# Second tile of each later pair transposed by small SBUF transfers and VectorE instead of TensorE

## The chip, the cores and the metric

The kernel runs on one core of one Trainium2 chip. A core has TensorE (PE in the profile; PEld is its loading of stationary operands), VectorE (DVE), ScalarE (ACT), GpSimd (POOL), and SyncE (SP), which here only issues DMA transfers. The metric is the device time of one execution in microseconds. Beside the plain timings there is one profiled execution, and all durations below come from its trace.

## The reference

The input `x` has two sequences of 1024 tokens with 1024 features, all float32. The block is pre-norm attention followed by a pre-norm feed-forward layer (FFN):

```
x = x + attention(layernorm(x))     # conv of width 3, 16 heads, blocks of 128 tokens, projection
x = x + ffn(layernorm(x))

ffn(x): y = x @ W_base.T + b_base   # 1024 x 1024
        z = x @ A[active].T         # 4 experts of rank 8
        alpha = softmax(log(prior[active]) + router logits[active])
        return y + 2 * sum_e alpha_e * (z_e @ B_e.T)
```

The change touches only the FFN, and in it only how the normalized tokens get their features onto the partitions, which the product with `W_base` needs.

## The kernel before, in words

The first 500 us do the convolution and attention. The last 250 us are the FFN, over the 2048 tokens as 16 tiles of 128 tokens, taken as 8 pairs, `m` = 0 to 7. A pair is a matrix of 256 tokens by 1024 features, seen as two by two blocks: A11 and A12 are the two feature halves of the first tile, A21 and A22 those of the second. The product with `W_base` uses seven block products in place of eight (Winograd's form). It needs the sums S1 = A21 + A22, S2 = S1 - A11, S3 = A11 - A21 and S4 = A12 - S2. Each block and sum is split into a high and a low float32r part (`op_hi` L1249 on ScalarE, `op_lo` L1252 on VectorE), and a block product is three times four matmuls of 512 columns (`multiply_half`, L1271).

For a pair TensorE does, in this order: the attention projection of the next pair's second tile (`project`, tile `pp`), product 1, the projection of the next pair's first tile, product 6, product 2, the eight transposes of the next pair's second tile, product 5, the expert and router products (`pz`), product 7, the eight transposes of the next pair's first tile, product 3, the small expert products, product 4. So each pair's operands are made while TensorE works at the pair before. Products 2 and 3 use the weight blocks B21 and B22, which do not stay in SBUF. `stream` fetches each of them again for every pair as two transfers of 1 MB (`load_half`, L1123, issued by SP) into two buffers of the tag `vh`, and product 3's B22 can be fetched only when product 2 has used up B21. The trace names both `wb_B`: the matmuls `py_a<-wb_B` are product 2, `py_e<-wb_B` product 3.

A tile's way to its operands is as follows. SP loads the residual (`load_xr`, L1171). GpSimd adds the projection's bias (`add_projb`, L1174), and later in two instructions the pair's common term (`add_u`, L1377 and L1379). VectorE adds the projection (`residual`, L1189), takes the moments (`x_stats`, L133 to L1194), GpSimd the reciprocal root (`x_rstd`, L1199), and VectorE writes the normalized tile `xn` (`x_norm`, L1204). TensorE then transposes eight blocks of 128 by 128 into two PSUM banks `trx` (`transpose_x`, L1211). Of the second tile, ScalarE copies A21 out of PSUM (`keep_a21`, L1233), and VectorE adds S1 from it and from A22 (`sum_s`, L1243). A result leaves PSUM by VectorE's `add_y` (L1385), and SP stores the tile (L1413). The gate of the experts (`gate_logits`, `gate_exp`, `gate`, L1315 to L1346) stands on VectorE and ScalarE between product 7 and the small expert products.

The order on all five engines is written by the kernel itself. Each piece of work is an `Op` with an engine, an estimated duration, a due time and its predecessors, and `trace()` sorts all of them by a small list scheduler and issues them. `places` counts free buffers by tag: `m` for the eight PSUM banks, `a4` for SBUF tiles of 4 KB a partition. `port=True` tells the scheduler that a VectorE and a GpSimd instruction must not overlap. A transfer takes one of eight completion counters of SP's queue in turn, and waits until the transfer eight places before it on that queue has landed. Every engine works strictly in its order.

Of the kernel before, what the change touches and what calls it, by code (L numbers as in the profile page):

```python
# [16 lines left out]
ALU = mybir.AluOpType  # L17
# [4 lines left out]
P = 128  # L22
# [17 lines left out]
def preln_block_kernel(  # L40
# [19 lines left out]
    nc = tc.nc  # L60
    N, L, D = x.shape
# [10 lines left out]
    E = lora_b.shape[0] // R  # L72
# [577 lines left out]
    DVE, ACT, PE, DMA = "DVE", "ACT", "PE", "DMA"  # L650
# [4 lines left out]
    loaded, gs, gone = {}, {}, {}  # L655
# [7 lines left out]
    at = [14.0]  # L663
# [3 lines left out]
    def turn(i, h):  # L667

        due = at[0]
        if h == 0:  # L670
            how = HOW[i]
            if how == "scalar":
                o = Op(ACT, 1.3, due - 8.0, 8.0, [loaded[i]], partial(ln_sum, i))
                o = Op(ACT, 1.2, due - 6.0, 8.0, [o], partial(ln_square, i))
                o = Op(DVE, 0.1, due - 4.5, 8.0, [o], partial(ln_variance, i), lag=1.8)
            else:
                lag = 1.0 if how == "vector" else 1.8
                o = Op(DVE, 1.6, due - 5.5, 8.0, [loaded[i]], partial(ln_stats, i), lag=lag)
            e, us = (DVE, 0.75) if how == "vector" else (ACT, 1.15)
            seen[i] = Op(e, us, due - 2.2, 8.0, [o], partial(ln_scale, i))  # L680
        o = Op(
            PE, TR, due, 6.0, [seen[i], banks[-2] if len(banks) > 7 else None],
            partial(transpose, i, h),
        )
        if (i, h) == (8, 0):

            gone["even"] = Op(
                DMA, 0.01, due - 2.0, 50.0, [seen["tr", j, 1] for j in range(8)], even_tokens
            )
        after = [o] + ([gone["even"]] if i > 7 else [])  # L690
        seen["tr", i, h] = o
        banks.append(Op(ACT, 0.52, due + TR, 8.0, after, partial(transposed, i, h)))
        at[0] += TR
        seen[i, h] = banks[-1]
# [36 lines left out]
    for q, (v, n, dc) in enumerate(units):  # L731
# [10 lines left out]
        o = Op(DVE, 1.28, due - 5.5, 9.0, took, partial(unit_sum, q))  # L742
        o = Op(ACT, 0.55, due - 3.5, 9.0, [o], partial(unit_hi, q))
        side = Op(DVE, 0.64, due - 1.5, 9.0, [o], partial(unit_lo, q))
        for i in range(2):
            d = dc + i
# [4 lines left out]
            for c in range(NCC):  # L751
                after = [last, side, ready[v, d]]
# [48 lines left out]
    for v, dc in [(v, dc) for v in (1, 2, 3) for dc in range(0, NDC, 2)] + [(4, 0), (4, 2)]:  # L801
        if (v, dc) == (2, 0):

            for r in range(4):
                load(
                    at[0] + r, 3.0, nc.sync.dma_start, mask[r::4], causal[ts(r, P // 4)],
                    after=[last],
# [4 lines left out]
        side = begin_step(v, dc, at[0])  # L812
# [18 lines left out]
    for c in range(NCC):  # L831
        got = load(
            at[0] - 4.0, 8.0, tokens_load, 0, c, t3, NV - 1,
            after=[gone["m", v, c] for v in (0, 5, 1, 2, 3)],
# [4 lines left out]
        o = Op(DVE, 2.7, at[0] + 1.0, 6.0, [got, gone[4, c]], partial(tokens_join, 0, c))  # L839
        o = Op(ACT, 0.6, at[0] + 4.0, 6.0, [o], partial(tokens_hi, 0, c))  # L840
# [23 lines left out]
    def a4(name, shape, dt=F32):  # L864
        return ap_.tile([P, *shape], dt, tag="a4", name=name, bufs=A4)
# [197 lines left out]
    NH = NDC // 2  # L1063
# [149 lines left out]
            xns.pop(g)  # L1213


    AT = {(0, 0): "A11", (0, 1): "A12", (1, 0): "A21", (1, 1): "A22"}

    def operand(m, n):
# [6 lines left out]
    def s_of(m, n):  # L1225

        k = m, n in ("S2", "S4")
        if k not in sums:
            sums[k] = a4(f"s{int(k[1])}_{m}", (2, NH, P))
        return sums[k][:, int(n in ("S3", "S4"))]  # L1230
# [3 lines left out]

    def sum_s(m, n):
        g0, g1 = gs[2 * m : 2 * m + 2]
        a, b, how = {
            "S1": (trxs.get((g1, 1)), s_of(m, "S3"), ALU.add),
            "S2": (s_of(m, "S1"), trxs.get((g0, 0)), ALU.subtract),
            "S3": (trxs.get((g0, 0)), s_of(m, "S3"), ALU.subtract),  # L1240
            "S4": (trxs.get((g0, 1)), s_of(m, "S2"), ALU.subtract),
        }[n]
        nc.vector.tensor_tensor(s_of(m, n), a, b, how)  # L1243
# [175 lines left out]
    MM = 1.37  # L1419
    LAG = 0.25  # L1420
    ROOM = 1.09
    NI = NCHUNK * NHP
    places.update(
        m=[0.0] * 8, t2=[0.0] * 6, t4=[0.0] * 6, a4=[0.0] * (A4 - 1), ml=[0.0] * 2, vh=[0.0] * 2,
# [3 lines left out]
    gs = [ch * NB + b for ch in (2, 3, 0, 1) for b in range(NB)]  # L1428
    d = {}

    def pe(key, takes, after, f, lead=8.0, need=("m",), give=()):
        d[key] = Op(PE, takes, at[0], lead, [d.get(a) for a in after], f, need=need, give=give)
        at[0] += takes
        return d[key]

    def op(key, e, takes, due, after, f, lead=14.0, **kw):
        if e in (DVE, ACT):
            kw.setdefault("lag", LAG)
            takes *= ROOM
        d[key] = Op(e, takes, due, lead, [d[a] for a in after if a in d], f, **kw)  # L1440
        return d[key]
# [93 lines left out]
    def plan_p(n):  # L1535
        g = gs[n]
        ch = g // NB
        plan_x(n, at[0])

        if ch < NCHUNK - 2 and g % NB == 1:  # L1540
            for wc in range(NWC):
                op(("oh", ch, wc), DMA, 1.4, at[0] - 8.0, [("os", ch, wc)], partial(load_oh, ch, wc),
                   lag=3.0, need=("t4",), lead=6.0)
                d["ol", ch, wc] = d["oh", ch, wc]
        for h in range(2):
            pe(("P", n, h), MM,
               [("ol", ch, wc) for wc in range(NWC)] + [("rl", "pw", wc, h) for wc in range(NWC)],
               partial(project, g, h), give=("t4",) * 2 if h and g % NB == NB - 2 else ())
            op(("r", n, h, 0), DVE, 0.6, at[0] + 0.5, [("P", n, h), ("xb", n)],
               partial(residual, g, h), give=("m",))  # L1550
        op(("xs", n), DVE, 1.6, at[0] + 2.0, [("r", n, 0, 0), ("r", n, 1, 0)], partial(x_stats, g))
        op(("xp", n), POOL, 0.3, at[0] + 3.5, [("xs", n)], partial(x_rstd, g), lag=0.3)
        op(("xn", n), DVE, 0.75, at[0] + 5.0, [("xp", n)], partial(x_norm, g), need=("a4",), port=True)

    def plan_tx(m, t, h):

        n, o = 2 * m + t, AT[t, h]
        pe(("TX", n, h), 0.44, [("xn", n)], partial(transpose_x, gs[n], h), give=("a4",) if h else ())
        d["A", m, o] = d["TX", n, h]
        due = at[0]  # L1560

        def more(key, e, takes, dt, after, f, **kw):
            op((key[0], m, *key[1:]), e, takes, due + dt, [(a[0], m, *a[1:]) for a in after], f, **kw)

        if o == "A21":
            more(("c", o), ACT, 0.5, 0.5, [("A", o)], partial(keep_a21, m), need=("a4",), give=("m",))
        else:
            more(("h", o), ACT, 0.5, 0.5, [("A", o)], partial(op_hi, m, o), need=("a4",))
            more(("l", o), DVE, 0.6, 1.2, [("h", o)], partial(op_lo, m, o))
        made = {n for n in ("A11", "A12", "A21", "A22") if ("A", m, n) in d}  # L1570

        def split(n, dt, after):
            more(("h", n), ACT, 0.5, dt, [("s", n)], partial(op_hi, m, n), need=("a4",))
            more(("l", n), DVE, 0.6, dt + 0.7, [("h", n)], partial(op_lo, m, n), port=True)

        def done(n, dt, after):
            more(("x", n), DVE, 0.0, dt, after, partial(drop, m, n), give=("m",))

        def free(n, dt, after):
            more(("f", n), DVE, 0.0, dt, after, int, give=("a4",))  # L1580

        if {"A21", "A22"} <= made and ("s", m, "S1") not in d:
            more(("s", "S1"), DVE, 0.6, 1.9, [("c", "A21"), ("A", "A22")], partial(sum_s, m, "S1"))
            done("A22", 2.0, [("s", "S1"), ("l", "A22")])
            split("S1", 3.0, [])
        if {"A11", "A21", "A22"} <= made and ("s", m, "S2") not in d:
            more(("s", "S2"), DVE, 0.6, 2.6, [("s", "S1"), ("A", "A11")], partial(sum_s, m, "S2"),
                 need=("a4",))
            more(("s", "S3"), DVE, 0.6, 3.3, [("s", "S1"), ("A", "A11")], partial(sum_s, m, "S3"))
            done("A11", 3.4, [("s", "S2"), ("s", "S3"), ("l", "A11")])  # L1590
            split("S2", 4.0, [])
            split("S3", 6.0, [])
            free(0, 7.0, [("l", "S1"), ("l", "S3"), ("s", "S2")])
        if len(made) == 4:
            more(("s", "S4"), DVE, 0.6, 4.0, [("s", "S2"), ("A", "A12")], partial(sum_s, m, "S4"))
            done("A12", 4.1, [("s", "S4"), ("l", "A12")])
            split("S4", 7.0, [])
            free(1, 8.0, [("l", "S2"), ("l", "S4")])
# [259 lines left out]
    plan_e(m, 0, 1, "e", [("Y", m, 3, 0)], sum_up=False)  # L1858

    for x in range(2):  # L1860
        pe(("Y", m, 3, 1 + x), 6 * 0.12, [("wl", "B22", 1, m)], partial(multiply_last, m, x), need=())
        op(("a", m, x), DVE, 0.35, at[0] + 0.3, [("Y", m, 3, 1 + x), ("pu", m, 0)], partial(add_last, m, x))
        op(("o", m, x), DMA, 0.4, at[0] + 0.7, [("a", m, x)], partial(store_last, m, x), lag=3.3)
    with tc.manual_schedule(
# [71 lines left out]
```

## Time and profile before

| | us |
|---|---|
| three runs, median (lowest, highest) | 753.68 (753.35, 755.99) |
| profiled execution, its own time | 752.35 |
| its span, first to last instruction | 750.5 |
| TensorE busy in the span | 741.9 |
| VectorE busy in the span | 596.3 |
| ScalarE / GpSimd busy in the span | 421.3 / 187.4 |
| TensorE clock granted | 0.999 of full |

Rows of groups give an instruction's line, engine, operation, output and inputs, shape and count, and then busy time, the mean of one, and the idle time before it with what ended it. Rows in order of time begin with the start and the duration in us from the start of the span; a bracket at their end tells how long the engine sat idle first and who released it. "SPq" rows are DMA issues of SP: their duration is that of the issuing instruction, not of the transfer.

### The profile page before, as it was taken

The page shows a single profiled execution, that of the slowest core. Times are in us where ns is not written, and L with a number is a line of the kernel's source. Part 1 is how long each engine was busy: PE and PEld are TensorE (multiplying, and loading weights), DVE is VectorE, ACT ScalarE, POOL GpSimd, SP SyncE. Part 2 cuts the span into 40 slices and gives each one's busy share as a digit, 9 for nine tenths or more (in the row PEclk, how much of TensorE's full clock was granted, in tenths as well). Part 3 has the DMA queues.
Part 4 walks back from the last instruction along what each step waited for, and adds up shares of the span by engine and source line. Part 5 has one row for each costly group of instructions (what it writes and reads, how often), then busy time and mean ns, then how long its engine had stood idle before and what let it go on. Part 6 is the DMA issues. An engine that isn't in the chain of part 4 may idle for free.

```text
span 750.5 us, 12939 instructions
## 1 busy us (share of the span) xinstructions
PE 741.9 (99%) x4746; PEld 633.9 (84%) x4746; DVE 596.3 (79%) x1051; ACT 421.3 (56%) x1044; POOL 187.4 (25%) x154
## 2 busy tenths in 40 slices
PE   8999999999999999999999999999999999999997
PEld 7999988888888888888888888888888888888886
DVE  6888899889767898898888888599667677577752
ACT  6888336464745998798898789863212212212120
POOL 3224321310000223132222312454142251331401
PEclk9999999999999999999999999999999999999999
DMA  9936994995753113363245344797655566565644
GB/s 342 379 104 206 248 267 107 292 287 124 249 167 127 44 50 103 132 220 103 99 153 206 131 151 138 266 386 317 227 211 225 215 238 235 209 225 217 227 174 168
DMA packets 65423, 149.46 MB, mean 199 GB/s; under 512 B 5918, under 2 KB 25006, under 8 KB 60240
## 3 DMA queue, kind: packets, MB, share of 16 engines
q1 hardware_dynamic: 61488, 138.51, 51.1%
q0 software_dynamic: 3728, 10.00, 7.4%
q8 instruction: 37, 0.61, 0.3%
q14 instruction: 26, 0.21, 0.1%
q10 hardware_dynamic: 144, 0.13, 0.1%
HBM read 114.01 MB, written 34.60 MB: 198 GB/s over the span
## 4 chain that ended last, share of the span: by engine, by line
PE 95%; DVE 2%; DMA 1%; ACT 1%; SPq 1%; issue 0%; DVEq 0%; ACTq 0%
PE pm L141 27%; PE pq L141 11%; PE py_c L1271 6%; PE pw L141 6%; PE py_a L1271 6%; PE pp L141 6%; PE py_e L1271 6%; PE pv L141 5%; PE po L978 4%; PE s L914 4%; PE pt L961 4%; PE py_b L1271 3%; PE pz L1288 2%; PE trx L1211 2%; PE tr L393 1%; DMA xt<-in_x 1%
## 5 line engine op out<-in xcount | busy, mean ns | idle before, releaser
L141 PE MATMUL pm<-v,u 128*128 128x256 f32 (+1 forms) x1152 | 203.1, 337 | 1.2 <-ACT v L481 0.6
L141 PEld LDWEIGHTS pm<-v,u 128*128 128x128 f32 x1152 | 177.8, 189 | 24.0 <-ACT v L481 0.9
L954 POOL TENSOR_TENSOR p<-p,rs 128x1024 f32<-128x1024 f32 x32 | 60.7, 1908 | 250.4 <-DVE rs L950 240.5
L943 ACT ACTIVATE p<-p,nmx 128x128 f32<-128x128 f32 x256 | 99.7, 398 | 4.3 <-DVE nmx L938 4.1
L141 PE MATMUL pq<-yt,wqk 128*128 128x512 f32 x384 | 94.6, 398 | 0.0
L141 PEld LDWEIGHTS pq<-yt,wqk 128*128 128x128 f32 x384 | 70.3, 188 | 16.8 <-issue 1.9
L1174 POOL TENSOR_TENSOR xr<-xr,projb 128x1024 f32<-128x1024 f32 x16 | 38.8, 2426 | 113.2 <-DMA xr<-in_x 104.7
L943 ACT ACTIVATION_READ_ACCUMULATOR p<-p,nmx 128x1 f32 x256 | 50.2, 196 | 0.0
L929 DVE TENSOR_TENSOR p<-s,mask 128x512 f32<-128x512 f32 x64 | 42.4, 685 | 9.7 <-PE s L914 9.5
L141 PE MATMUL pw<-oT,wot 128*128 128x512 f32 x192 | 47.9, 397 | 0.0
L141 PE MATMUL pv<-wvt,yt 128*128 128x512 f32 x192 | 47.1, 395 | 0.0
L141 PEld LDWEIGHTS pv<-wvt,yt 128*128 128x128 f32 x192 | 36.0, 188 | 8.8
L141 PEld LDWEIGHTS pw<-oT,wot 128*128 128x128 f32 x192 | 35.9, 188 | 8.7 <-DVE oT L999 0.2
L431 POOL DMA_DIRECT2D g<-in_conv_w x24 | 21.3, 938 | 69.9 <-ACT g L427 36.2
L453 DVE TENSOR_TENSOR u<-g,u 128x768 fp32r<-128x768 f32 x40 | 37.5, 953 | 1.5 <-ACT u L449 1.4
L969 DVE COPY pT<-pt 128x512 f32<-128x512 f32 x32 | 21.8, 688 | 20.8 <-PE pt L961 20.8
L938 DVE TENSOR_REDUCE nmx<-p 128x8 f32<-128x1024 f32 x32 | 37.7, 1196 | 0.1
L1233 ACT COPY s<-trx 128x512 f32<-128x512 f32 x8 | 4.7, 588 | 56.9 <-PE trx L1211 56.9
L449 ACT CAST u<-g 128x768 fp32r<-128x768 f32 x40 | 32.7, 838 | 5.2 <-PE pm L141 4.8
L914 PEld LDWEIGHTS s<-qk,qk 64*128 64x128 f32 x512 | 30.1, 187 | 5.1 <-issue 2.3
L914 PE MATMUL s<-qk,qk 64*128 64x128 f32 x512 | 34.0, 280 | 0.0
L1369 ACT COPY u<-py_a 128x512 f32<-128x512 f32 x8 | 4.7, 588 | 51.9 <-PE py_a L1271 51.9
(206 smaller groups left out, 1532.6 us busy)
## 6 DMA issues: line engine op xcount, KB each, us to landing
wb_B<-wsd_B SPq DMA_DIRECT2D x32, 1024.0 KB, 7.1
g<-in_conv_w SPq DMA_DIRECT2D x48, 384.0 KB, 8.3
mdr<-m SPq DMA_DIRECT2D x36, 256.0 KB, 3.0
g<-in_conv_w POOLq DMA_DIRECT2D x24, 384.0 KB, 7.3
xt<-in_x SPq DMA_DIRECT2D x16, 512.0 KB, 9.8
xr<-in_x SPq DMA_DIRECT2D x16, 512.0 KB, 5.6
out<-xr SPq DMA_DIRECT2D x14, 512.0 KB, 6.5
ml<-mdr SPq DMA_DIRECT2D x18, 384.0 KB, 4.0
```

The lines of the kernel that those rows point to most:

```text
L141: nc.tensor.matmul(ps, l[a], r[b], start=first and i == 0, stop=last and i == 2)
L449: nc.scalar.copy(us[v, dc][0], raws[v, dc])
L453: nc.vector.tensor_tensor(lo, raws.pop((v, dc)), hi, ALU.subtract)
L914: nc.tensor.matmul(s[j][:, b, :], qh[ts(j, DH), ts(b, P)], kh[ts(j, DH), ts(b, P)], start=True, stop=True,)
L929: nc.vector.tensor_tensor(ps[i][0][:, ts(j, NB), :], ss[i][j], mask[:, None, :].to_broadcast([P, NB, P]), ALU.add,)
L938: nc.vector.tensor_reduce(nmx, p, AX.X, ALU.max, negate=True)
L943: nc.scalar.activation(p[:, k, :], p[:, k, :], AF.Exp, bias=nmx[:, k : k + 1], accum_out=sm[:, k : k + 1],)
L954: nc.gpsimd.tensor_tensor(p, p, rs[:, :, None].to_broadcast([P, 2 * NB, P]), ALU.mult)
L961: nc.tensor.transpose(pt[:, ts(b, P)], ps[i][0][:, j * NB + b, :], ident)
L978: nc.tensor.matmul(po[ts(j, DH), ts(b, P)], vh[:, b, ds((i % 4) * P + j * DH, DH)], pT[:, j, ts(b, P)], start=True, stop=True,)
L1174: nc.gpsimd.tensor_tensor(xrs[g], xrs[g], pwt["b"], ALU.add)
L1271: nc.tensor.matmul(pys[m, b], l[x], r[y], start=opens and c == 0 and i == 0, stop=c == NH - 1 and i == 2, skip_group_check=not opens,)
```

## The change

For the second tile of pairs 1 to 7 (seven tiles) TensorE's eight transposes are left out. In their place SP issues sixteen transfers from SBUF to SBUF per tile (`spread`). Each moves 32 partitions by 8 runs of 32 features, a run being 128 bytes, 32 KB in all. Together they put block (q, a) of the four by four grid of 32 by 32 blocks in each 128-feature group at the place of block (a, q). Then VectorE transposes each 32 by 32 block in place of it, with two instructions of 128 by 512 (`turn`), back into the tile `xn`. The blocks A21 and A22 then lie in SBUF and not in PSUM. The copy of A21 by ScalarE goes, the sums and splits read SBUF, and a few bookkeeping entries of the scheduler follow. The tile `xp` between the two steps is one more buffer of tag `a4`. The scheduler orders all engines anew from these entries. In the program that it writes, SP's sixteen transfers stand together, right ahead of the two transfers of B22, in all seven pairs. VectorE's two transposes stand next to the gate's instructions, ahead of them in most pairs and behind them in the others. The splits and sums of A22 and S1, which stood between products 5 and 7, now stand behind the transposes.

```
+    def spread(g, a):
+        if a == 0:
+            xps[g] = a4(f"xp_{g}", (D,))
+        src = xns[g].rearrange("p (c a f) -> p c a f", a=QB, f=32)
+        dst = xps[g].rearrange("p (c q f) -> p c q f", q=QB, f=32)
+        for q in range(QB):
+            nc.sync.dma_start(dst[ts(a, 32), :, q], src[ts(q, 32), :, a])
+    def turn(g, h):
+        t = xns[g][:, ts(h, 512)]
+        nc.vector.transpose(t, xps[g][:, ts(h, 512)])
+        trxs[g, h] = t.rearrange("p (c j) -> p c j", c=NH)
...
     def sum_s(m, n):
+        a21 = trxs[g1, 0] if (g1, 0) in trxs else s_of(m, "S3")
-            "S1": (trxs.get((g1, 1)), s_of(m, "S3"), ALU.add),
+            "S1": (trxs.get((g1, 1)), a21, ALU.add),
-            "S3": (trxs.get((g0, 0)), s_of(m, "S3"), ALU.subtract),
+            "S3": (trxs.get((g0, 0)), a21, ALU.subtract),
...
+    XD = 1.4
...
+        if n > 1 and n % 2 == 1:
+            for a in range(QB):
+                op(("xd", n, a), DMA, XD, at[0] + 2.5 + XD * a, [("xn", n), ("xd", n, 0)], partial(spread, g, a),
+                   lag=5.0 if a else 0.0, need=("a4",) if a == 0 else ())
...
-        pe(("TX", n, h), 0.44, [("xn", n)], partial(transpose_x, gs[n], h), give=("a4",) if h else ())
+        side = m > 0 and t == 1
+        if not side:
+            pe(("TX", n, h), 0.44, [("xn", n)], partial(transpose_x, gs[n], h), give=("a4",) if h else ())
+        else:
+            op(("TX", n, h), DVE, 0.6, at[0] - 1.5 + 0.7 * h, [("xd", n, a) for a in range(QB)],
+               partial(turn, gs[n], h), give=("a4",) if h else ())
...
-        if o == "A21":
+        if o == "A21" and side:
+            d["c", m, o] = d["A", m, o]
+        elif o == "A21":
             more(("c", o), ACT, 0.5, 0.5, [("A", o)], partial(keep_a21, m), need=("a4",), give=("m",))
...
-        pe(("Y", m, 3, 1 + x), 6 * 0.12, [("wl", "B22", 1, m)], partial(multiply_last, m, x), need=())
+        pe(("Y", m, 3, 1 + x), 6 * 0.12, [("wl", "B22", 1, m), ("E", m, 0, 1), ("Y", m, 3, x)], partial(multiply_last, m, x), need=())
```

The last lines only add predecessors to the two last product pieces of the final pair, so that their order stays as it was.

More of the change, by code (lines that the diff above doesn't have):

```diff
@@ L1213, in transpose_x @@
             xns.pop(g)
+    QB = P // 32
+    xps = {}
+    def spread(g, a):
[9 more added lines that the diff above has]
+        trxs[g, h] = t.rearrange("p (c j) -> p c j", c=NH)
+        if h == 1:
+            xns.pop(g)
+            xps.pop(g)
     AT = {(0, 0): "A11", (0, 1): "A12", (1, 0): "A21", (1, 1): "A22"}
@@ L1568, in plan_tx @@
             more(("h", o), ACT, 0.5, 0.5, [("A", o)], partial(op_hi, m, o), need=("a4",))
-            more(("l", o), DVE, 0.6, 1.2, [("h", o)], partial(op_lo, m, o))
+            more(("l", o), DVE, 0.6, 1.2, [("h", o)], partial(op_lo, m, o), port=side)
         made = {n for n in ("A11", "A12", "A21", "A22") if ("A", m, n) in d}
@@ L1576, in done @@
         def done(n, dt, after):
-            more(("x", n), DVE, 0.0, dt, after, partial(drop, m, n), give=("m",))
+            give = ("m",) if m == 0 or n != "A22" else ()
+            more(("x", n), DVE, 0.0, dt, after, partial(drop, m, n), give=give)
         def free(n, dt, after):
@@ L1582, in plan_tx @@
         if {"A21", "A22"} <= made and ("s", m, "S1") not in d:
-            more(("s", "S1"), DVE, 0.6, 1.9, [("c", "A21"), ("A", "A22")], partial(sum_s, m, "S1"))
+            more(("s", "S1"), DVE, 0.6, 1.9, [("c", "A21"), ("A", "A22")], partial(sum_s, m, "S1"),
+                 need=("a4",) if m else (), port=m > 0)
             done("A22", 2.0, [("s", "S1"), ("l", "A22")])
@@ L1589, in plan_tx @@
             more(("s", "S3"), DVE, 0.6, 3.3, [("s", "S1"), ("A", "A11")], partial(sum_s, m, "S3"))
+            if m:
+                more(("x", "A21"), DVE, 0.0, 3.4, [("s", "S3"), ("x", "A22")], partial(drop, m, "A21"),
+                     give=("a4",))
             done("A11", 3.4, [("s", "S2"), ("s", "S3"), ("l", "A11")])
```

## The prediction

> **What bounds the kernel now.** I read the page first: busy times and the chain that ended last.
>
> ```profile
> PE 741.9 (99%) x4746; PEld 633.9 (84%) x4746; DVE 596.3 (79%) x1051; ACT 421.3 (56%) x1044; POOL 187.4 (25%) x154
> ...
> PE 95%; DVE 2%; DMA 1%; ACT 1%; SPq 1%; issue 0%; DVEq 0%; ACTq 0%
> ```
>
> TensorE is the bound. The second view is the table by stretches, for one pair of the FFN, and then the chain in order of time around a removed step:
>
> ```profile
> 570.00:600.00 30.00, 30.00 (x166) 25.05 (x165) 21.73 (x43) 5.64 (x12) 9.45 (x6) 1.00 0.64 243
> ```
>
> ```profile
> 582.74 2.77 PE py_a L1271 x12
> 585.52 0.87 PE trx L1211 x8
> 586.39 2.81 PE py_e L1271 x12
> ```
>
> The columns of the first are PE, PEld, DVE, ACT, POOL, then clock, DMA share and GB/s. TensorE has no idle microsecond in the pair, so eight transposes taken away are worth their place in the chain, as long as everything that TensorE needs stays in time. What may come late is read from the timeline:
>
> ```profile
> 573.21 2.39 POOL L1174 TENSOR_TENSOR xr<-xr,projb 128x1024 f32<-128x1024 f32 x1 [15.07 <-DMA xr<-in_x]
> 573.27 2.88 DVE L1252 TENSOR_TENSOR S<-s,S 128x512 fp32r<-128x512 f32 x1
> ...
> 582.08 0.81 DVE L1204 TENSOR_SCALAR xn<-xr,lnmv_b,lnrs_b 128x1024 f32<-128x1024 f32 x1
> 584.16 1.71 SPq L1123 DMA_DIRECT2D wb_B<-wsd_B  x2
> 585.13 1.03 PEld L1211 LDWEIGHTS trx<-identr,xn 128*128 128x128 f32 x8
> 586.12 2.64 PEld L1271 LDWEIGHTS py_e<-wb_wr,S 128*128 128x128 f32 x12
> 595.11 2.61 PEld L1271 LDWEIGHTS py_e<-wb_B,S 128*128 128x128 f32 x12
> ```
>
> The second tile's `xn` ends at 582.89. SP issues B22's two halves from 584.16, as product 2 frees them. Product 3 starts on them at 595.11. In the new order sixteen transfers stand on SP between `xn` and these two. That is the place which decides.
>
> **The gain.** A removed tile of transposes is 0.87 us in the chain, and 585.13 to 586.12, 0.99 us, from its first load of weights to the next product's. I take 0.95. Seven tiles: 6.6 us (ends 6.1 and 6.9). ScalarE's seven copies of A21 (0.59 us each) and two PSUM banks per pair are freed too. They are worth nothing, ScalarE being busy 5.64 of 30 us.
>
> **The room for sixteen issues.** The span from the second tile's `xn` to product 3 is, in the timeline's rows, 14.3 us in pair 0, 12.2 in pairs 1 and 2, and 15.1 to 15.3 in pairs 3 to 6. Of it go 0.95 (product 3 comes sooner), the time until B22 has landed, and an estimated 0.15 for semaphores between engines:
>
> ```profile
> DMA to landing us min/median/max: 4.7/7.1/9.5
> ```
>
> This is the row of `wb_B`. The two halves are issued together, the first lands in the smallest value, 4.7, the second in the middle one, 7.1. Product 3 needs the second only half a product later, 1.4 us. So the second binds, with 7.1 - 1.4 = 5.7 us. That leaves 7.5, 5.4, 5.4 and four times 8.4 us.
>
> **VectorE makes `xn` later.** The trace before has no transpose of VectorE. The nearest row is its copy of one PSUM bank, 128x512 at 688 ns, 0.64 apart in a row of several. I take two at 0.64, 1.3 us per tile (ends 1.1, and 2.4 if 4-byte values pass twice). Three operations (A22's split, S1's sum and split, 1.9 us) move from a stretch in which VectorE idled to the dense one after product 7. So the next tile's `xn` has 3.2 us more ahead of it. In the dense stretch VectorE now loses 2.3 us: the instruction at 573.27 takes 2.88 in place of 0.64 because GpSimd holds the port they share until 575.60. That loss is the cover. It takes all but 0.9, and I put `xn` 1.0 later from pair 1 on (ends 0 and 3.3). The room becomes 7.5, 4.4, 4.4, and four times 7.4.
>
> **What the sixteen cost on SP.** No transfer of this form is in the trace. Near rows:
>
> ```profile
> 0.73 1.80 SPq L253 DMA_DIRECT2D xt<-in_x  x4
> L557 SPq DMA_DIRECT2D ml<-mdr x24: 360/530/587, 204.8 to 421.6; - x24
> L653 SPq DMA_DIRECT2D mask<-in_causal x4: 564/610/650, 105.8 to 134.6; - x4
> ```
>
> Lower end: plain transfers of one run a partition, four in a row in 1.80 us, 0.45 each; 0.33 if they reach the 0.32 of a single one. Upper end: 32 partitions, as here, 0.61 and about 0.05 to the next, 0.66. Nearest in form is `ml`, with several runs in each partition: 0.53. Sixteen: 8.5 us. They exceed the room by 1.0, 4.1, 4.1 and four times 1.1 us, 13.6 in all. Product 3 waits that long, with all of TensorE behind it.
>
> The ninth waits for the first one's landing (counters, eight in turn). The smallest landing in the trace is 2.0 us and eight issues take 4.2, so this is free.
>
> **What they cost on the DMA engines.** A tile is 4096 runs of 128 bytes, 256 per engine. In the trace's packet records a packet of 512 bytes takes 27 ns, of 1 KB 46, of 4 KB 159: about 8 ns and 37 per KB. That makes 13 ns for 128 bytes and 3.3 us per tile, hidden behind the 8.5 of issue. Even at the 27 ns of 512 bytes it is 6.9, still hidden. Two rules of the Trainium skill stand here, both in "DMA: Bandwidth & Descriptors". "Why small descriptors are slow (HBM only)" says that transfers from SBUF to SBUF keep 78% of the link with packets of 128 bytes. With its 435 GB/s an estimate of 1.5 us per tile, below my row's value, and the sum is the same 7.0 us. "Rules for kernel authors" speaks against the change: below 64 KB one pays mostly overhead, and "Anatomy of one DMA" puts the fixed part near 2.0 us. With eight in flight that is an estimated 4.0 us a tile, hidden too; only one after another, 32 us, would it stop the kernel by some 24 us a pair. I go by the rows, and by issue, not bytes.
>
> **What waits for `turn`.** VectorE's first transpose waits for all sixteen. In pair 2 the last lands at 583.9 + 8.5 + 2.2 = 594.6, and VectorE comes there at about 594.3, so it stands some 0.3 us, the gate's instructions with it where they are behind. The gate's result, needed at 597.7 before, then comes about 0.5 us late against an unstalled TensorE. The 4.1 us of waiting for B22 hide it; without this cover it would cost that 0.5. B21 and the residual behind B22 on SP are needed 15 and 6 us after their issue, which covers them.
>
> **Sum.** -6.6 + 13.6 = +7.0 us on the profiled execution's 752.35 (span 750.5 and 1.9 around it): 759.4. The median of the runs lies 1.3 above that execution, so 760.7 us.
>
> **Rivals.** *SP issues at the pace of single transfers* (other side: faster). At 0.33, 5.3 us, only pairs 1 and 2 stall, 0.9 each: -6.6 + 1.8 = -4.8, 748.9; 747.1 if `xn` is not later. At 0.45, the four in a row, 7.2 us: -6.6 + 2 x 2.8 = -1.0, 752.7. It decides at 16 issues in 7.5 us, 0.47 each, where the stalls equal the gain. For it: nearly every single transfer on SP reads 0.32 to 0.33. Against: the `ml` and `mask` rows.
>
> *The pace of `mask`*: 0.66, 10.6 us, stalls 3.1 + 2 x 6.2 + 4 x 3.2 = 28.3: +21.7, 775.4. Its 32 partitions speak for it, its strided destination against.
>
> *VectorE and GpSimd as the new bound*: A22 and A21 now come from SBUF, so more of VectorE's instructions have both inputs there and meet GpSimd's 2.4 us instructions, as at 573.27. If `xn` itself falls behind one, it is 2.4 us later. In six pairs that adds 14.4: 775.1. Against: VectorE has 8 us idle in a pair.
>
> *Small packets*: above 8.5 us for 256 runs, 33 ns a run, the engines, not SP, are the limit. At 60 ns, 15.4 us a tile, the stalls are 7.9 + 2 x 11 + 4 x 8 = 61.9: +55, 809. No packet size in the trace points there.
>
> **How the numbers follow.** Pace 0.49 to 0.60 (755 to 769, likeliest): 0.37. Pace of single transfers, to 0.36 (747 to 750): 0.30. Between the two: 0.14. Pace of `mask`: 0.08. Port: 0.06. Packets: 0.05. A measurement of this kernel tells about 0.5%, 3.8 us, from no change: faster is below 749.9, slower above 757.4. Of the single pace 0.02 and of the likeliest 0.03 fall within that bound, with the 0.14: same 0.19, faster 0.28, slower 0.53. The range, 747 to 775, leaves out packets and the very ends. The likeliest case alone is 755 to 769.
>
> **What would show it.** Right: seven tiles of `trx` gone from TensorE; a wait of product 3 (`py_e<-wb_B`) for the transfer `wb_B` of about 4 us in pairs 1 and 2 and about 1 in the others; SP's rows of `xp` standing 0.5 to 0.6 apart; `wb_B`'s first half issued right behind the sixteenth. Wrong: `xp` rows 0.45 apart or less and no idle before product 3, then the gain is kept; `wb_B` landing much later than 5 us after its issue, then the engines are full; TensorE idle before `pzt` for the gate, then `turn` is what is late; or idle before `pp` or `py_b`, then VectorE is.

## The result, and the profile after

The changed kernel takes 788.55 us (median; 785.42 to 788.94), the kernel before 753.54 (753.35 to 755.99). The ratio is 1.0448, with a 95% interval from 1.0413 to 1.0482. That is 35 us slower, outside the range of the prediction. The profiled execution took 785.42 us, with a span of 783.6 against 750.5: 33.1 us more. It is the fastest of the four; the readings below are of this execution and its 33.1 us.

The busy times and the chain that ended last, of the changed kernel:

```profile
PE 750.2 (96%) x4690; PEld 637.8 (81%) x4690; DVE 600.8 (77%) x1065; ACT 418.1 (53%) x1037; POOL 189.1 (24%) x154
...
PE 78%; DMA 6%; SPq 6%; DVE 6%; ACT 2%; issue 2%; POOL 0%; DVEq 0%; ACTq 0%; POOLq 0%
```

Two things are to be seen here. The chain now runs over SP's queue and over a DMA for 12% of the span, which was 2% before. And TensorE has 56 instructions fewer (4690 for 4746) but is busy 8.3 us longer. So it not only waits, it also works more slowly.

The waits of TensorE in the FFN (total, times, longest) and one stretch of 30 us, with the columns of the row shown before:

```profile
PE py_e L1295 <- DMA wb_B<-wsd_B: 24.8, 7, 4.8
```

```profile
570.00:600.00 30.00, 25.99 (x120) 21.15 (x119) 21.05 (x41) 4.72 (x9) 10.01 (x6) 0.94 0.60 221
```

All waiting is in one place: product 3 waits for B22, once in each of the seven pairs, 24.8 us in all. The granted clock of this stretch is 0.94, where it was 1.00. Around one of these waits (pair 2), in order of time:

```profile
591.85 0.80 DVE L1204 TENSOR_SCALAR xn<-xr,lnmv_b,lnrs_b 128x1024 f32<-128x1024 f32 x1
...
592.73 10.39 SPq L1227 DMA_DIRECT2D xp<-xn  x16
...
603.22 1.02 SPq L1123 DMA_DIRECT2D wb_B<-wsd_B  x2
...
604.30 1.03 PE L1211 MATMUL trx<-identr,xn 128*128 128x128 f32 x8
...
608.35 2.70 PE L1295 MATMUL py_e<-wb_B,S 128*128 128x512 f32 x6 [3.02 <-DMA wb_B<-wsd_B]
```

SP starts on the sixteen when `xn` is there, and is busy with them for 10.39 us. B22 leaves right behind, at 603.22, and product 3 starts on it 5.1 us later. Then six matmuls take 2.70 us, where six at full clock take 1.6. The rows of the new instructions (shortest, middle and longest duration in ns) give the pace:

```profile
L1227 SPq DMA_DIRECT2D xp<-xn x112: 597/608/1610, 520.3 to 742.3; - x112
L1232 DVE STREAM_TRANSPOSE xn<-xp x14: 668/686/712, 533.2 to 746.1; 128x512 f32<-128x512 f32 x14
```

An issue takes 0.61 us, and from its start to the start of the next it is 0.65. The sixteen take 10.4 us in four tiles. In three others a single issue is longer (0.93 to 1.61 us) and they take 10.7 to 11.4. That is 75.2 in all.

The slower work shows when the wait of pair 0 is cut into stretches (PE busy is the first number after the length, the clock is the third from the end):

```profile
530.08:533.49 3.41, 3.41 (x22) 2.92 (x21) 0.83 (x4) 0.27 (x2) 0.00 (x0) 1.00 0.43 63
533.49:536.90 3.41, 0.34 (x4) 0.10 (x1) 3.25 (x13) 1.63 (x3) 0.00 (x0) 1.00 0.94 384
536.90:543.73 6.83, 6.20 (x16) 4.80 (x17) 1.26 (x3) 0.49 (x2) 0.00 (x0) 0.50 0.55 206
543.73:570.00 26.27, 26.27 (x144) 21.75 (x142) 20.12 (x32) 3.61 (x8) 10.32 (x6) 1.00 0.46 154
```

After a stretch of 3.41 us in which TensorE hardly worked, the granted clock is 0.50 for the next 6.83 us. Matmuls of 512 columns then start 0.427 us apart, where it is 0.231 at full clock. Over the FFN TensorE worked 27.6 us at half clock. At these two paces that costs 27.6 x (1 - 0.231/0.427) = 12.7 us.

The sum of the measured parts: 24.8 (waiting) + 12.7 (half clock) - 6.0 (56 transposes, 0.108 us from one to the next in the trace) = 31.5, against 33.1 more in the span. What the other 1.6 us are is not settled; 0.6 of them go if the transposes are worth only the 5.4 us of the first experiment below.

### The profile page after: what moved, and what is told of

Its sections match the earlier page's. It is cut to its first block, busy times and chain, and to the rows that moved or that the text cites. A ratio compares the mean times of both kernels' runs of the same rounds, so it can differ in the third digit from the quotient of the medians.

```text
span 783.6 us, 13015 instructions
## 1 busy us (share of the span) xinstructions
PE 750.2 (96%) x4690; PEld 637.8 (81%) x4690; DVE 600.8 (77%) x1065; ACT 418.1 (53%) x1037; POOL 189.1 (24%) x154
## 4 chain that ended last, share of the span: by engine, by line
PE 78%; DMA 6%; SPq 6%; DVE 6%; ACT 2%; issue 2%; POOL 0%; DVEq 0%; ACTq 0%; POOLq 0%
PE pm L141 25%; PE pq L141 11%; PE py_e L1295 5%; PE pw L141 5%; SPq L1227 5%; PE pv L141 5%; DMA wb_B<-wsd_B 5%; PE py_c L1295 4%; PE po L978 4%; PE s L914 4%; PE pt L961 3%; PE pp L141 3%; PE py_a L1295 3%; PE py_b L1295 1%; PE tr L393 1%
## 5 line engine op out<-in xcount | busy, mean ns | idle before, releaser
L1295 PE MATMUL py_e<-wb_B,S 128*128 128x512 f32 x90 | 32.9, 520 | 24.8 <-DMA wb_B<-wsd_B 24.8
L1276 DVE TENSOR_TENSOR S<-s,S 128x512 fp32r<-128x512 f32 x32 | 24.4, 791 | 39.1 <-ACT S L1273 39.1
L1324 ACT COPY zk<-pz 72x256 f32<-72x256 f32 x8 | 2.9, 368 | 88.6 <-PE pz L1312 88.6
L1295 PEld LDWEIGHTS py_e<-wb_B,S 128*128 128x128 f32 x90 | 21.8, 250 | 31.3 <-DMA wb_B<-wsd_B 15.2
```

What stands on the lines that cost most here:

```text
L1295: nc.tensor.matmul(pys[m, b], l[x], r[y], start=opens and c == 0 and i == 0, stop=c == NH - 1 and i == 2, skip_group_check=not opens,)
```

## The experiments

The theory after the result: the issue time of sixteen transfers on SP delays B22, TensorE waits for it, and the wait itself halves the clock afterwards. The rivals were full DMA engines, VectorE's later work, and a low clock with some other cause.

### No transfers, VectorE's work kept

```
     def spread(g, a):
         if a == 0:
             xps[g] = a4(f"xp_{g}", (D,))
-        ...
-            nc.sync.dma_start(dst[ts(a, 32), :, q], src[ts(q, 32), :, a])
...
-        nc.vector.transpose(t, xps[g][:, ts(h, 512)])
+        nc.vector.transpose(t, t)
```

> Leaves the sixteen transfers out; VectorE transposes xn in place, so the second tile's operands hold other data. All else, and every other instruction's place, as in the changed kernel. Theory (the transfers ahead of B22 on SP cost everything): no idle before product 3, clock full, 753.5 - 6.6 = about 747 us. Rival (VectorE's later work also costs): TensorE idle in front of products 1, 6 or the projection, 750 us or more.

Measured: 748.16 us, ratio 0.9941 (0.9921 to 0.996), clock 1.000, span 745.1. The waits of TensorE in the FFN come to one line:

```profile
PE pzt L1372 <- DVE zr L1366: 0.4, 1, 0.4
```

All that VectorE has more to do, and the new order on VectorE and ScalarE, thus cost almost nothing. The whole loss lies with the transfers. What the removed transposes are worth is read here too: 5.4 us in the span, and a pair of 29.5 us in place of 30.3.

### The same runs in four transfers

```
-        for q in range(QB):
-            nc.sync.dma_start(dst[ts(a, 32), :, q], src[ts(q, 32), :, a])
+        nc.sync.dma_start(dst[:, :, a], src[:, :, a])
```

> The same 4096 runs of 128 bytes per tile, but in four transfers of 128 partitions by 8 runs (each block stays on its partitions, so the operands hold other data). Theory of issue time: four issues of 0.6 us, 2.4 us, or up to 1.3 us each if the number of runs counts; B22 goes out 5 to 8 us sooner, little or no idle before product 3, 746 to 751 us. Rival (the DMA engines are full of small packets, B22 queues behind them): the idle before product 3 stays near 3.5 us a pair, 780 us or more.

Measured: 747.35 us, ratio 0.9932 (0.991 to 0.9953). TensorE waits for nothing in the FFN, at clock 1.000. SP's row:

```profile
L1226 SPq DMA_DIRECT2D xp<-xn x28: 605/672/1575, 520.2 to 699.5; - x28
```

The DMA engines move the same 4096 runs of 128 bytes per tile as in the changed kernel. So neither the bytes nor the small packets are the matter, but the number of issues. One with four times the runs takes 0.67 us, hardly more than 0.61. This is a test and no remedy: with four transfers no block changes its partitions, so the exchange that the change needs is left out.

### Sixteen transfers of one run a partition

```
-            nc.sync.dma_start(dst[ts(a, 32), :, q], src[ts(q, 32), :, a])
+            nc.sync.dma_start(dst[ts(a, 32), 0, q], src[ts(q, 32), 0, a])
...
-        nc.vector.transpose(t, xps[g][:, ts(h, 512)])
+        nc.vector.transpose(t, t)
```

> Sixteen transfers of 32 partitions as before, but one run of 128 bytes in each partition in place of eight; VectorE transposes xn in place (other data). If an issue costs 0.6 us whatever it moves: pitch 0.65 us, stalls as in the changed kernel or some 0.9 us a pair shorter because the engines are empty when B22 comes, 776 to 789 us. If the number of runs sets the cost of an issue: pitch 0.33 to 0.4, at most 1 us of idle in pairs 1 and 2, 746 to 750 us.

Measured: 783.98 us, ratio 1.0406 (1.0386 to 1.0426). SP's row, and then the waits:

```profile
L1227 SPq DMA_DIRECT2D xp<-xn x112: 512/588/1550, 521.0 to 741.2; - x112
```

```profile
PE py_e L1295 <- DMA wb_B<-wsd_B: 20.2, 7, 4.9
PE py_e L1295 <- DVE s L1267: 3.7, 1, 3.7
```

An eighth of the bytes makes an issue 0.02 us shorter and the kernel 4.6 us faster. The other 30 us are still there. The two runs together take the two ends: same bytes with few issues is fast, few bytes with the same issues is slow.

### TensorE kept at work during the wait

```
         if opens and h == 0:
             pys[m, b] = bank(f"py_{b}_{m}")
+        if k == 3 and h == 0 and m < NM - 1:
+            w0 = bank(f"warm_{m}")
+            for i in range(14):
+                nc.tensor.matmul(w0, wb["B11", 0][:, 0, 0, :P], wb["B11", 0][:, 0, 0, :], start=True, stop=True)
```

> The changed kernel with 14 matmuls of 128x512 on resident weights into a spare PSUM bank, 3.2 us, ahead of product 3 in pairs 0 to 6; their results are not used. They fill most of the idle time. Theory (the idle time itself closes TensorE's clock to half for 3.4 us or more after it): the half-clock stretches go, up to 14 us come back, less up to 1 us a pair because the second half of B22 binds next to a full-speed product 3: 772 to 780 us. Rival (the low clock has nothing to do with the idle time): clock stays at 0.94 in the FFN, 786 to 795 us.

Measured: 776.29 us, ratio 1.0323 (1.0296 to 1.0351), 12.3 below the changed kernel, though TensorE has 98 matmuls more to do. The waits that are left:

```profile
PE py_e L1299 <- DMA wb_B<-wsd_B: 2.9, 5, 1.3
PE py_e L1299 <- DVE s L1267: 1.2, 1, 1.2
```

No stretch of half clock is left in the FFN. The filling (7 x 3.2 = 22.4 us) and the remaining waits (4.1) take 26.5 us, about as long as the waiting did before (24.8). So B22 comes no earlier, and what came back is the clock. Of the loss, this much is shown to come from the wait's after-effect and not from its length.

### B22 ahead of the sixteen

`stream(m, "B22")` is called before product 5's operands are planned, and the sixteen get its second half as a predecessor. Their duration is told as 2.0 us per four, and VectorE's transposes are due later.

```
+        stream(m, "B22", 4.0)
+        plan_spread(2 * m + 3)
         for h in range(2):
             plan_tx(m + 1, 1, h)
...
-        stream(m, "B22")
...
+               [("xn", n), ("xd", n, 0), ("wl", "B22", 1, n // 2 - 1)], partial(spread, gs[n], a),
```

> The same sixteen transfers, planned behind B22's two halves on SP (and with due times to match); everything is computed. Theory (only their place ahead of B22 costs): no idle before product 3, clock full, the gain of 6 to 7 us is kept, 746 to 749 us. Rival (they delay whatever stands behind them): VectorE's transposes now wait until about 12 us after product 2, the gate or S2's parts come late, or B21 and the stores behind the sixteen do: TensorE idle in front of pzt, py_b or py_a, 755 us or more.

Measured: 757.74 us, ratio 1.0049 (1.0026 to 1.0072). The rival was right. Product 3 waits no more, and product 2 does, for B21:

```profile
PE py_a L1295 <- DMA wb_B<-wsd_B: 9.1, 6, 3.1
```

```profile
534.45 5.81 SPq L1227 DMA_DIRECT2D xp<-xn  x9
540.67 0.34 SPq L1171 DMA_DIRECT2D xr<-in_x  x1
541.12 0.36 SPq L1437 DMA_DIRECT2D out<-xr  x1
541.53 0.42 SPq L1171 DMA_DIRECT2D xr<-in_x  x1
542.07 1.27 SPq L1437 DMA_DIRECT2D out<-xr  x1
543.43 17.26 SPq L1123 DMA_DIRECT2D wb_B<-wsd_B  x4
```

The first of these four is B21's. It leaves at 543.43, behind all sixteen (the first row has the nine that end in the stretch shown), two residuals and two stores; in the kernel before it left at 536.12. Two of the waits were long enough to halve the clock.

### Only the planned duration changed

```
-    XD = 1.4
+    XD = 2.6
```

> The changed kernel with one number changed: the planner is told 2.6 us per four transfers (16 x 0.65 measured) in place of 1.4. It then puts B22's halves ahead of the sixteen in pairs 2 to 6. Theory: no idle before product 3, the clock stays full; what is behind the sixteen (residual, stores, then B21) comes later, as in the run with B22 first: some idle before product 2 where B21's issue waits behind stores, 748 to 758 us. Rival (planning is not the matter): 775 us or more.

Measured: 764.05 us, ratio 1.0136 (1.011 to 1.0161). It lies between what the two sides expected, nearer to the theory. Told the measured time, the planner itself puts B22 ahead of the sixteen in most pairs, and 24.5 us of the loss go. Then several others are late:

```profile
PE py_a L1295 <- DMA wb_B<-wsd_B: 4.2, 3, 2.8
PE pzt L1376 <- DVE zr L1370: 2.9, 1, 2.9
PE py_e L1295 <- DMA wb_B<-wsd_B: 2.4, 2, 2.0
PE pp L141 <- DMA oht<-ohd: 2.1, 2, 1.4
PE trx L1211 <- DVE xn L1204: 1.3, 1, 1.3
```

### Another queue

First all sixteen on ScalarE's queue, with VectorE's transposes due later, then eight on each (the lines for the second):

```
         for q in range(QB):
-            nc.sync.dma_start(dst[ts(a, 32), :, q], src[ts(q, 32), :, a])
+            e = nc.sync if q < 2 else nc.scalar
+            e.dma_start(dst[ts(a, 32), :, q], src[ts(q, 32), :, a])
```

> All sixteen on ScalarE's queue. If only SP's queue matters: 746 to 750 us. If an issue holds up any engine that it stands on: 10.4 us of ScalarE in one piece, while zk, A22's split and the gate's exponential wait behind them; TensorE idle for ScalarE or for what follows from it, 762 to 785 us.

Measured: 806.39 us, ratio 1.0697 (1.0639 to 1.0756), worse than either side expected. The small copy `zk` waits behind the sixteen, and TensorE for it:

```profile
PE pzs L1329 <- ACT zk L1324: 28.0, 7, 7.9
PE py_a L1386 <- ACT zT L1380: 2.9, 6, 0.8
PE pzt L1376 <- DVE zr L1370: 2.9, 2, 1.6
```

So the cost of an issue is not one of SP's alone: on ScalarE's queue its middle duration is 0.62 us. On both it is time in order, and what it costs the kernel depends on who stands behind.

> Eight of the sixteen on SP ahead of B22 as in the changed kernel, eight on ScalarE's own queue. SP then needs 8 x 0.65 = 5.2 us against a room of 7.4 (pair 0 and 3 to 6) or 4.4 us (pairs 1 and 2): idle of 0.8 us in two pairs, too short for the clock to fall, 747 to 750 us. Rival (ScalarE's 5.2 us of issuing holds up its copies): TensorE idle before pzs, py_b or py_e for ScalarE, 753 us or more.

Measured: 750.08 us, ratio 0.9955 (0.9937 to 0.9973), clock 1.000. The rows of the transfers on both queues, and the waits:

```profile
L1227 SPq DMA_DIRECT2D xp<-xn x56: 585/609/1544, 522.3 to 704.9; - x56
L1227 ACTq DMA_DIRECT2D xp<-xn x56: 592/628/1887, 522.3 to 705.2; - x56
```

```profile
PE py_e L1295 <- DMA wb_B<-wsd_B: 0.9, 2, 0.5
PE pzt L1376 <- DVE zr L1370: 0.6, 1, 0.6
PE py_a L1386 <- ACT zT L1380: 0.5, 1, 0.5
```

Both queues issue at once at almost the pace that each has alone (0.61 and 0.63 us). With 5.2 us on SP the room nearly suffices: 0.9 us of waiting for B22 is left. This version is faster than both kernels and keeps 3.6 of the 5 to 6 us.

### The sixteen on SP, B22 on ScalarE

```
+            side = w == "B22" and m < len(gs) // 2 - 1
-            op(("wl", w, h, m), DMA, 2.75, ...
+            op(("wl", w, h, m), *((ACT, 0.35) if side else (DMA, 2.75)), ...
```

> All sixteen stay on SP, B22's two halves are issued by ScalarE in pairs 0 to 6 (two short issues that wait for product 2 there), the sixteen's duration is given to the planner as 2.6 us per four, and VectorE's transposes are due later, behind the gate. Everything is computed. Theory: B22 goes out as soon as product 2 frees B21, no idle before product 3, B21 in time as the sixteen start early: 746 to 749 us. Rival (counters are shared by both queues, so a B22 half waits for a small transfer eight places before it; or the sixteen meet B22 in the engines): idle before product 3 or 2, 752 us or more.

Measured: 758.48 us, ratio 1.0062 (1.0025 to 1.0098). The rival's side again. Of the seven spans from one product 3 to the next four are 29.4 to 29.5 us, as hoped, and the others 30.4 to 33.2:

```profile
PE py_a L1295 <- DMA wb_B<-wsd_B: 4.8, 2, 3.7
PE pp L141 <- DMA oht<-ohd: 2.4, 3, 1.5
```

```profile
582.59 14.96 SPq L1227 DMA_DIRECT2D xp<-xn  x16
597.60 1.08 SPq L1034 DMA_DIRECT2D oht<-ohd  x2
```

In pair 2 the sixteen took 14.96 us on SP, and the operand `oht` of the next projection stood behind them. The trace says why these took 15 and not 10.4: SP stood 3.9 us, in two waits, until earlier ones of the sixteen had landed. The chain of this stretch has one of them under way from 583.89 to 591.73. B22's two halves had been issued on ScalarE at 582.85 and 584.24, and of the packets of 128 bytes next to none moved from 584.5 to 587. So here the small transfers did meet B22 in the DMA engines, as the rival said. In the changed kernel, where B22 leaves behind the sixteen, SP has no such wait.

> The kernel before, with only B22's halves moved to ScalarE's queue in the same way: the control for the last run. Theory: TensorE was never idle there, so no change, ratio 0.998 to 1.002. Rival (the other queue itself helps): below 0.997.

Measured: 753.13 us against 752.65, ratio 1.0002 (0.9983 to 1.0021). Moving B22 is worth nothing in itself.

### What makes an issue dear

Sixteen transfers of another form in each pair:

```
+            o, k = {
+                3: (d[:, f], s[:, f]),
+                5: (d[r, w], s[ts((a + 1) % QB, 32), w]),
+                7: (d[:, w], s[:, w]),
+                9: (d[r, w], x0[r, w]),
+                11: (d[:, w], x0[:, w]),
+                13: (d[r, ts(q, 32)], s[r, ts(q, 32)]),
+                15: (d[ts(a // 2, 64), f], s[ts(1 - a // 2, 64), f]),
+            }[n]
+            nc.sync.dma_start(o, k)
```

> Sixteen transfers per tile in the place of the changed kernel's, but of another form in each pair, none of them used (VectorE transposes xn in place, other data): SBUF to SBUF with 128 partitions of 128 bytes, 32 of 1 KB, 128 of 1 KB; HBM to SBUF with 32 partitions of 1 KB, 128 of 1 KB; SBUF to SBUF with 32 of 128 bytes on their own partitions; 64 of 128 bytes. Read are only SP's durations per form. If 32 partitions make an issue dear: 0.55 to 0.6 in the 2nd, 4th and 6th form, 0.32 to 0.4 in the others. If SBUF as the source does: 0.55 to 0.6 in all but the 4th and 5th. If standing in a row does: near 0.4 to 0.6 in all.

SP's rows of them in order of time, one a pair:

```profile
521.43 10.67 SPq L1239 DMA_DIRECT2D xp<-xn  x16
...
557.99 10.10 SPq L1239 DMA_DIRECT2D xp<-xn  x16
...
592.07 10.17 SPq L1239 DMA_DIRECT2D xp<-xn  x16
...
621.73 7.43 SPq L1239 DMA_DIRECT2D xp<-in_x  x16
...
650.68 11.68 SPq L1239 DMA_DIRECT2D xp<-in_x  x16
...
686.34 10.06 SPq L1239 DMA_DIRECT2D xp<-xn  x16
...
719.63 10.09 SPq L1239 DMA_DIRECT2D xp<-xn  x16
```

The rows of the 2nd and 4th form, both 32 partitions of 1 KB, from SBUF and from HBM:

```profile
L1239 SPq DMA_DIRECT2D xp<-xn x16: 582/589/597, 558.0 to 567.5; - x16
```

```profile
L1239 SPq DMA_DIRECT2D xp<-in_x x16: 311/420/431, 621.7 to 628.7; - x16
```

All five forms from SBUF to SBUF have a middle duration of 0.59 to 0.60 us, with 32, 64 or 128 partitions, 128 bytes or 1 KB. The two from HBM have 0.42 (the fifth form's 11.68 holds waits of 4.7 us in all, for landings of the same sixteen). So in these forms the source decides, not the partitions. In a row, such a load from HBM takes 0.42 where a single one takes 0.32.

A source in SBUF alone is not enough. In the kernel before, transfers from SBUF to HBM are issued as fast as single loads:

```profile
L530 SPq DMA_DIRECT2D mdr<-m x36: 319/327/1681, 60.4 to 230.7; - x36
```

So what is dear here has both ends in SBUF. Standing in a row is not the reason: the first of the sixteen, 3 to 8 us after the issue before it, takes 0.60 us or more in the changed kernel. Nor are all loads from HBM cheap: the prediction's rows of `ml` and `mask`, both from HBM, have 0.53 and 0.61. No run varied what sets these two apart.

## Why the prediction was wrong

The place was right: B22 waiting on SP behind sixteen issues, with TensorE behind it, and nothing else on the path. Two steps failed.

*What the sixteen cost on SP.* I took 0.53 each, from `ml`, because of its several runs in each partition. Measured: 0.65, and 75.2 us for the seven tiles (2.4 of it in the three long issues), not 7 x 8.5 = 59.5. The number of runs hardly counts (0.59 for one, 0.61 for eight); that both ends lie in SBUF does. None of my three rows was such a transfer, so the nearest row was none. The rival at the pace of `mask` had the right size by luck: its reason was the 32 partitions, and 32 partitions of 1 KB from HBM take 0.42.

*"Product 3 waits that long, with all of TensorE behind it."* I priced a wait at its length. It costs the clock as well: 12.7 us, more than my whole sum. This term was missing, in the rivals too, and so the `mask` rival came to 775.4 and not to 788. In the trace before TensorE waits for nothing in the FFN, and the clock falls only at the very end, where its work runs out (0.97 in the stretch from 720 to 750.5). The Trainium skill states the rule, in "TensorE: Matmul & The Clock Gate", part 1: half clock is the state after an idle window of about 3.4 us, and a busy window brings full clock back. I did not weigh this rule. By it, my own waits of 4.1 us in pairs 1 and 2 could each have cost half of 3.4 us on top, an estimate, and those of 1.1 us nothing. The runs are harsher than the page: the wait of pair 6, 2.3 us, halved the clock as well.

The other steps, by their terms:

| step | predicted | measured |
|---|---|---|
| 56 transposes gone | -6.6 us | -5.4 to -6.0 us (runs without and with four transfers); 0.87, the chain's row, was the better one than 0.99 |
| `xn` later, summed over seven tiles | 6.0 us | 5 to 6 us, in part by luck: up to 1.4 earlier in pairs 0 to 2 and 0.9 to 3.2 later in 3 to 6, where 1.0 later was expected in each from pair 1 on |
| B22 from issue to product 3 | 5.7 us, by its second half | 5.0 to 5.75, by its first half; in pairs 1 to 6 half of product 4 stands between the two halves |
| waiting for B22 | 13.6 us | 24.8 us |
| VectorE's transposes | 0.64 us from one to the next | 0.63 to 0.64 us (0.69 long, as the copy of a bank) |
| waiting of `turn` | hidden | hidden: no wait of `pzt` |
| small packets, port | nothing | nothing (four transfers; no transfers). A packet of 128 bytes took 13 ns, as worked out from the rows; the estimate of 1.5 us a tile from the page's rate would make it 6, so the measured figure stands |
| fixed part of a transfer | near 2.0 us by the page's "Anatomy of one DMA" | 2.0 us is the smallest landing on SP's queue in the trace before; the page fits its figure on transfers that GpSimd issues |

With 0.65 in place of 0.53 the sum of waits becomes 27, near the measured 24.8. With the clock added (27 + 12.7 - 6.6 = 33) it is close to the result. That waiting for a counter is free held but for three single issues of 0.93 to 1.61 us; what these waited for, the trace does not show.

The rival on the other side needed less than 0.47 us an issue and was never near. That the gain is there when the issues are not in the way is shown by the runs with four transfers and with eight on each queue.

## What to carry to other kernels

Count DMA issues as instructions of the engine that issues them: a step that replaces 0.9 us of TensorE by sixteen issues needs 10 us of somebody's order, and whoever stands behind them is late. Moving them behind one victim makes another (B22, then B21, then `oht` or `zk`); fewer and larger transfers, where the layout allows them, or a split over two queues, take most of the cost away. Only the split was shown with the exchange of partitions kept. The split is what the Trainium skill's "Perfetto Trace Analysis", section "DMA Optimizations", advises for a queue that is solid with issues. And when a forecast has TensorE wait for more than about 2 us, add the clock to the price: here 2.3 us were enough.

## What the runs showed of the hardware

- An issue of a transfer from SBUF to SBUF takes 0.59 to 0.61 us on SP, 0.63 on ScalarE, in all shapes tried here (0.67 for 128 partitions of 8 runs). One from SBUF to HBM takes 0.32 (`mdr`). From HBM to SBUF a single one takes 0.32 and a plain one in a row 0.42, but `ml` took 0.53 and `mask` 0.61. SP and ScalarE issue at the same time without slowing each other much (0.61 and 0.63).
- The clock is decided in a fixed grid of stretches of 3.41 us: its 15 changes in the changed kernel's FFN lie whole multiples of 3.41 us apart. In the FFN of the changed kernel and of the experiments, 32 such stretches at full clock, those at the end of the program left out, were followed by half clock: TensorE had been idle in them for 1.73 to 3.41 us. All full-clock stretches with less than 1.7 us of idle time (the longest had 1.59) were followed by full clock, and so was one with 1.78, near the end of a run. So about half a stretch is enough, where the Trainium skill speaks of an idle window. Full clock came back after a stretch at half clock with at most 0.6 us idle; with 0.5 us or more it mostly stayed at half for one more.
